# Joint layer-norm steps with their inverse roots on POOL

## The chip, the cores and the metric

The kernel runs on one core of a Trainium2 chip. The metric is device time in microseconds for one execution: the median of three runs before the change is 1777.33 us (1776.58 to 1781.38).

## What is computed

The input is 8 sequences of 2048 tokens with 256 features, float32. Three residual sublayers follow each other:

```python
x = x + 0.5 * ffn(layernorm(x), w1, b1, w2, b2)
x = x + s4d(layernorm(x), ...)        # a long convolution, then a layer norm of its own
x = x + 0.5 * ffn(layernorm(x), w1, b1, w2, b2)
```

`ffn` is `relu(x @ w1 + b1) @ w2 + b2` with an inner width of 1024, and `layernorm(x)` is `(x - mean) / sqrt(var + 1e-5)` over the 256 features of a token. Every layer norm therefore needs one inverse root for every token.

## The kernel before, in words

The 16384 tokens are split into 64 groups of 256 tokens (two tiles of 128 tokens, one token to a partition). The work runs in three stages: the first feed-forward sublayer with tag `a` (until some 800 us), the convolution, and the second feed-forward sublayer with tag `b`. In a feed-forward sublayer a group has eight slots, one for each 128 columns of the inner width. In a slot TensorE runs six "up" matmuls into `ph` (L856, each product split into a high and a low part of the operands), ACT makes `hx` by a relu (L928), DVE makes its low part (L116 on `hx`), and three slots later TensorE runs six "down" matmuls from `hx` into `po` (L866).

A group has a `pre` part before its up matmuls and a `post` part behind its down matmuls. Both are generators that the loop `sublayer` advances by one step in each slot; a bare `yield` in them is thus a wait of one slot. `pre` starts 18 slots ahead of the group's first up matmul in stage `a`. It loads `xa`, takes mean and variance on DVE (`bn_stats`, `bn_aggr` into `mv`), normalises into `xn` on ACT (L730), and turns `xn` by 128x128 transposes on TensorE (L794), or for some groups by two DMAs, into `xh` and `xl`, which the up matmuls read. POOL adds the output bias to `xa` (L777).

`post` of stage `a` adds `po` to `xa` and makes the second layer norm of the same rows, into `u`, for the convolution. The `post` of group g and the `pre` of group g+3 come together in time. From group 3 on they share one "joint" step (61 of them): one `mv` tile of 128x4 holds the mean and variance of both, and the inverse root is taken once for the four columns: a root on ACT (L704, `s_u`), then on DVE a reciprocal (L714), two steps that refine it (L116, `q_u`), a second reciprocal (L717) and the shift `nb_u` (L116). ACT's norms of `xn` and `u` (L730) read `t_u` and `nb_u`. Three numbers of a joint say in which slot, counted from `post`, the root, the refinement and the norm come: 2, 3, 4 for groups turned by DMA, else 3, 4, 6. In this text joint j is the one of `post` group j and `pre` group j+3.

Beside the matmuls of stage `a`, the tables for the convolution are built as background work: `matrices` with its inner `powers` (L490 to L497), `lags` (L536 to L570) and `make` (L600 to L610) put 285 multiplications, additions and small DMAs on POOL, most of them on tiles of 128x512, until about 568 us; ACT and DVE copy the tables (L620, L646) and SP moves them. After that POOL runs a scan (L1110 to L1113).

The order on each engine is not the order of the source alone. A scheduler that plans with its own timeline places each instruction, and each engine then takes its instructions strictly in that order. `keep_in_program_order` ties an instruction behind the one that was traced before it on the same engine; an instruction that is not tied may be placed on either side of it.

Of the kernel before, what the change touches and what calls it, by code (L numbers as in the profile page):

```python
# [10 lines left out]
F32 = mybir.dt.float32  # L11
# [4 lines left out]
ALU = mybir.AluOpType  # L16
# [3 lines left out]
P = 128  # L20
EPS = 1e-5
# [22 lines left out]
def macaron_s4d_kernel(  # L44
# [18 lines left out]
    V = nc.vector  # L63
    A_ = nc.scalar
    G_ = nc.gpsimd
# [10 lines left out]
    NTB = 2  # L76
    TOK = NTB * P
    NG = NJ * B // NTB
# [20 lines left out]
    const = ctx.enter_context(tc.tile_pool(name="const", bufs=1))  # L99
    stat = ctx.enter_context(tc.tile_pool(name="stat", bufs=4))  # L100
# [14 lines left out]
    def stt(o, a, s, b, op0, op1):  # L115
        return V.scalar_tensor_tensor(out=o, in0=a, scalar=s, in1=b, op0=op0, op1=op1)  # L116
# [10 lines left out]
    u = upool.tile([P, NQ, H, CQ], F32, name="u")  # L127
# [16 lines left out]
    hb2 = const.tile([P, H], F32, name="hb2")  # L144
    eps4 = const.tile([P, 1], F32, name="eps4")
    V.memset(eps4, 0.25 * EPS)
    A_.activation(stat.tile([P, 1], F32, name="warm", tag="s"), eps4, AF.Sqrt)

    W1Q = [nc.sync] * 4
# [536 lines left out]
    def moments(n, name):  # L686
        return stat.tile([P, n, 2], F32, name=f"mv_{name}", tag=f"mv{n}")

    def stats(srcs, name, pin=False, mv=None):
        st = stat.tile([P, NTB, 6], F32, name=f"st_{name}", tag="st")  # L690
        mv = moments(NTB, name) if mv is None else mv
        for i, src in enumerate(srcs):
            ins = V.bn_stats(st[:, i, :], src)
            if pin:
                tc.keep_in_program_order(ins)
        for i in range(NTB):
            V.bn_aggr(mv[:, i, :], st[:, i, :])
        return mv

    def root(mv, name):  # L700

        n = mv.shape[1]
        s = stat.tile([P, n], F32, name=f"s_{name}", tag=f"s{n}")
        root_[0] = A_.activation(s, mv[:, :, 1], AF.Sqrt, bias=eps4, scale=0.25)  # L704
        return s

    root_ = [None]

    def rstds(mv, s, name):

        n = mv.shape[1]
        t = stat.tile([P, n], F32, name=f"t_{name}", tag=f"tt{n}")
        q = stat.tile([P, n], F32, name=f"q_{name}", tag=f"q{n}")
        V.reciprocal(t, s)  # L714
        stt(q, mv[:, :, 1], EPS, t, ALU.add, ALU.mult)
        stt(q, q, 0.25, s, ALU.mult, ALU.add)
        V.reciprocal(t, q)  # L717
        return t

    def shifts(mv, rs, name):  # L720
        nb = stat.tile([P, mv.shape[1]], F32, name=f"nb_{name}", tag=f"nb{mv.shape[1]}")
        stt(nb, mv[:, :, 0], -1.0, rs, ALU.mult, ALU.mult)
        return nb

    def norm(dsts, srcs, mv, rs, name, on_act=False, nb=None, pin=False):
        if on_act and nb is None:
            nb = shifts(mv, rs, name)
        for i, (dst, src) in enumerate(zip(dsts, srcs)):
            if on_act:
                ins = A_.activation(  # L730
                    dst, src, AF.Identity, bias=nb[:, i : i + 1], scale=rs[:, i : i + 1]
                )
                if pin:
                    tc.keep_in_program_order(ins)
            else:
                V.tensor_scalar(dst, src, mv[:, i, 0:1], rs[:, i : i + 1], ALU.subtract, ALU.mult)
# [9 lines left out]
    def ucols(g):  # L746
        return [column(g * NTB + i) for i in range(NTB)]

    def halves(xt):
        return [xt[:, i, :] for i in range(NTB)]  # L750
# [215 lines left out]
    class Joint:  # L966
# [3 lines left out]
        def __init__(self, g, by_dma):  # L970
            self.mv = moments(2 * NTB, f"j{g}")

            self.root_at, self.rstd_at, self.norm_at = (2, 3, 4) if by_dma else (3, 4, 6)

    joints = {}
    JG = 3
# [13 lines left out]
    def post_a(g, po):  # L990
        xt = xts.pop(g)
        V.tensor_add(xt, po, xt)
        nc.sync.dma_start(out=x1_dram[:, g * NTB : (g + 1) * NTB, :], in_=xt)
        joint = joints.pop(g, None)
        mv = stats(halves(xt), f"u{g}", mv=joint.mv[:, NTB:] if joint else None)
        whole = joint.mv if joint else mv
        for _ in range(joint.root_at if joint else 1):
            yield
        s = root(whole, f"u{g}")
        if joint or g == NG - 1:  # L1000
            tc.keep_in_program_order(root_[0])
        for _ in range(joint.rstd_at - joint.root_at if joint else 1):
            yield
        rs = rstds(whole, s, f"u{g}")
        nb = shifts(whole, rs, f"u{g}")
        if joint:
            joint.rs, joint.nb = rs, nb
            rs, nb = rs[:, NTB:], nb[:, NTB:]

        for _ in range(joint.norm_at - joint.rstd_at + 1 if joint else 1):  # L1010
            yield
        for i in range(NTB):
            norm(
                ucols(g)[i : i + 1], [xt[:, i, :]], mv[:, i : i + 1], rs[:, i : i + 1], f"u{g}_{i}",
                g < ACT_NORM, nb[:, i : i + 1], True,
            )
            yield
        posted[0] = g + 1
# [199 lines left out]
    def begin():  # L1218
        for _ in range(sizes[1] // PB):
            next(head)  # L1220

    sublayer(
        w1t, w2t, pre_a, post_a, 18, "a", load_weights(), chain(matrices(), early()),
        {"half": NG // 2, "tables": NG * 3 // 4},
        {NG * SLOTS - 6: lambda: next(head), NG * SLOTS - 1: begin},
# [127 lines left out]
```

## Time and profile before

| | |
|---|---|
| median of the runs | 1777.33 us |
| the profiled execution | 1773.09 us, its span 1771.3 us |
| busy share of the span | PE 98%, DVE 78%, ACT 56%, POOL 33% |
| POOL busy from 200 to 400 us | 169.11 of 200 us |
| POOL busy from 600 to 800 us | 48.84 of 200 us |
| mean granted TensorE clock | 0.992 |

A row of a group reads: line, engine, operation, written tile <- read tiles, shape, count, then the time that the engine was busy with them, the mean duration of one in ns, and the idle time of the engine just ahead of them with what ended it. A row of the timeline reads: start, duration, engine, line, operation, tiles, shape, count, and in brackets the idle time before it. A row of the windows reads: the stretch, its length, then for each engine the busy time and the number of instructions, the granted TensorE clock, the share of the DMA engines and GB/s.

### The profile page before, as it was taken

What the parts mean: (1) busy time and instruction counts of PE and PEld (TensorE: products, weight loads), DVE (VectorE), ACT (ScalarE), POOL (GpSimd) and SP (SyncE); (2) the same over time, 40 slices, a digit from 0 to 9 for tenths busy, and PEclk for the clock granted to TensorE, in tenths of its full rate; (3) what the DMA queues carried; (4) which work ended last, traced back from release to release, by engine and by line L of the source; (5) the groups of instructions that cost most, each with busy time, mean ns of one, the idle gap of its engine ahead of it and who ended that gap; (6) DMA issues with size and microseconds to landing.
All of it is one profiled execution on the core that took longest, in us unless ns stands there. A gap on an engine that the chain in (4) does not pass through costs nothing. (4 is left out here: it accounts for less than half of the span.)

```text
span 1771.3 us, 41152 instructions
## 1 busy us (share of the span) xinstructions
PE 1729.9 (98%) x15411; PEld 1701.7 (96%) x15411; DVE 1373.3 (78%) x4415; ACT 997.8 (56%) x2188; POOL 591.5 (33%) x548
## 2 busy tenths in 40 slices
PE   8999999999999999999999899999999999999998
PEld 7999899999999999999999789999999999999998
DVE  6998777677766766766999678887788788888874
ACT  4554567667777755543555445555555555555553
POOL 1116979976776115110000122222222222222220
PEclk9999999999999999999999989999999999999999
DMA  5111266679877643335888913333333333333331
GB/s 194 43 49 40 72 203 209 192 214 288 249 233 238 173 114 94 93 108 170 260 268 260 290 49 90 94 92 91 90 96 96 90 88 93 90 96 96 90 96 49
DMA packets 299407, 245.33 MB, mean 139 GB/s; under 512 B 169924, under 2 KB 242372, under 8 KB 298694
## 3 DMA queue, kind: packets, MB, share of 16 engines
q1 hardware_dynamic: 297456, 241.75, 46.5%
q8 instruction: 121, 1.98, 0.5%
q0 software_dynamic: 768, 0.66, 0.2%
q14 instruction: 80, 0.66, 0.1%
q10 hardware_dynamic: 982, 0.27, 0.1%
HBM read 91.89 MB, written 111.15 MB: 115 GB/s over the span
## 5 line engine op out<-in xcount | busy, mean ns | idle before, releaser
L866 PE MATMUL po_a<-wa,hx_a 128*128 128x256 f32 x3072 | 455.8, 285 | 12.8 <-DVE hx_a L116 12.6
L856 PE MATMUL ph_a<-xh_a,wa 128*128 128x256 f32 x2048 | 455.1, 287 | 1.8 <-ACT xh_a L803 1.4
L856 PE MATMUL ph_b<-xh_b,wb 128*128 128x256 f32 x2048 | 444.9, 285 | 3.5 <-ACT xh_b L803 3.5
L866 PE MATMUL po_b<-wb,hx_b 128*128 128x256 f32 x3072 | 441.3, 283 | 0.1
L866 PEld LDWEIGHTS po_a<-wa,hx_a 128*128 128x128 f32 x3072 | 406.3, 193 | 15.9 <-DVE hx_a L116 15.1
L866 PEld LDWEIGHTS po_b<-wb,hx_b 128*128 128x128 f32 x3072 | 401.0, 192 | 0.3 <-DVE hx_b L116 0.3
L856 PEld LDWEIGHTS ph_a<-xh_a,wa 128*128 128x128 f32 x2048 | 356.1, 193 | 4.9 <-ACT xh_a L803 1.8
L856 PEld LDWEIGHTS ph_b<-xh_b,wb 128*128 128x128 f32 x2048 | 354.4, 194 | 4.1 <-ACT xh_b L803 4.1
L928 ACT ACTIVATE hx_b<-ph_b 128x256 fp32r<-128x256 f32 x512 | 193.8, 383 | 263.6 <-PE ph_b L856 249.6
L928 ACT ACTIVATE hx_a<-ph_a 128x256 fp32r<-128x256 f32 x512 | 192.9, 387 | 212.9 <-PE ph_a L856 206.0
L116 DVE SCALAR_TENSOR_TENSOR hx_a<-ph_a,hx_a 128x256 fp32r<-128x256 f32 x512 | 207.9, 412 | 129.1 <-ACT hx_a L928 127.7
L856 PE MATMUL ph_a<-xl_a,wa 128*128 128x256 f32 x1024 | 291.6, 286 | 3.4 <-DVE xl_a L837 3.1
L856 PE MATMUL ph_b<-xl_b,wb 128*128 128x256 f32 x1024 | 286.4, 285 | 0.0
L116 DVE SCALAR_TENSOR_TENSOR hx_b<-ph_b,hx_b 128x256 fp32r<-128x256 f32 x512 | 211.8, 415 | 66.9 <-ACT hx_b L928 61.5
L1288 POOL TENSOR_TENSOR xb<-xb,lnb_sb 128x512 f32<-128x512 f32 x64 | 82.5, 1292 | 502.1 <-DMA xb<-x_dram 332.4
L856 PEld LDWEIGHTS ph_a<-xl_a,wa 128*128 128x128 f32 x1024 | 198.2, 194 | 4.7 <-DVE xl_a L837 3.7
L856 PEld LDWEIGHTS ph_b<-xl_b,wb 128*128 128x128 f32 x1024 | 198.5, 194 | 0.2 <-DVE xl_b L805 0.2
L777 POOL TENSOR_TENSOR xa<-xa,hb 128x512 f32<-128x512 f32 x64 | 88.9, 1389 | 270.8 <-ACT xn L730 259.6
L777 POOL TENSOR_TENSOR xb<-xb,hb 128x512 f32<-128x512 f32 x64 | 94.6, 1477 | 62.5 <-ACT xn L730 31.8
L730 ACT ACTIVATE xn<-xb,nb_fb,t_fb 128x255 f32<-128x255 f32 x127 | 69.4, 594 | 75.4 <-DVE nb_fb L116 74.2
L815 DVE COPY pl_b<-xn 128x512 uint16<-128x512 uint16 x62 | 39.8, 642 | 74.8 <-ACT xn L730 74.8
L730 ACT ACTIVATE u<-xa,nb_u,t_u 128x256 f32<-128x256 f32 x104 | 89.9, 865 | 0.0
(262 smaller groups left out, 2537.8 us busy)
## 6 DMA issues: line engine op xcount, KB each, us to landing
xa<-in_L_attn_x_dram SPq DMA_DIRECT2D x64, 256.0 KB, 3.1
x_dram<-xa SPq DMA_DIRECT2D x64, 256.0 KB, 2.5
o<-u SPq DMA_DIRECT2D x32, 512.0 KB, 3.6
pv<-planes SPq DMA_DIRECT2D x32, 512.0 KB, 3.5
pt<-u SPq DMA_DIRECT2D x32, 512.0 KB, 3.9
tz<-kpad SPq DMA_DIRECT2D x64, 256.0 KB, 4.5
xb<-x_dram SPq DMA_DIRECT2D x64, 256.0 KB, 2.8
out_dram<-xb SPq DMA_DIRECT2D x64, 256.0 KB, 2.9
```

The costliest lines, as they stand in the source:

```text
L116: return V.scalar_tensor_tensor(out=o, in0=a, scalar=s, in1=b, op0=op0, op1=op1)
L730: ins = A_.activation(dst, src, AF.Identity, bias=nb[:, i : i + 1], scale=rs[:, i : i + 1])
L777: return G_.tensor_add(xt, xt, hb2.unsqueeze(1).to_broadcast([P, NTB, H]))
L815: copy(pl[:, w], xu[:, :, :, :, w])
L856: nc.tensor.matmul(ph, wt[wp][:, dc, fs], xp[:, dc, :], start=(n == 0), stop=(n == 3 * NDC - 1))
L866: nc.tensor.matmul(po[:, i, :], hp[:, tsl], wt[wp][:, fc, :], start=(fc == 0 and i == 0 and n == 0), stop=(fc == NFC - 1 and n == 2), skip ...
L928: last[A_] = A_.activation(hh, ph, AF.Relu)
L1288: G_.tensor_add(xt, xt, lnb_sb.unsqueeze(1).to_broadcast([P, NTB, H]))
```

## The change

The joint steps no longer use ACT's root or DVE's five small operations. Four operations on POOL take their place: add epsilon to the variances, raise to the power -1/2 with a constant 128x4 tile `power`, multiply by the means, and multiply by -1. All four are tied to the program order. The step comes in slot 1 (groups turned by DMA) or 2 after `post`, where the root came in slot 2 or 3; the norm stays in slot 4 or 6, and the later norm of `u` stays in its slot too. Norm steps outside the 61 joints keep the root on ACT.

```diff
+    power = const.tile([P, 2 * NTB], F32, name="power")
+    V.memset(power, -0.5)
...
+    def powers_of(mv, name):
+
+        n = mv.shape[1]
+        t = stat.tile([P, n], F32, name=f"t_{name}", tag=f"tt{n}")
+        nb = stat.tile([P, n], F32, name=f"nb_{name}", tag=f"nb{n}")
+        pin = tc.keep_in_program_order
+        pin(G_.tensor_scalar_add(t, mv[:, :, 1], EPS))
+        pin(G_.tensor_tensor(t, t, power, op=ALU.pow))
+        pin(G_.tensor_mul(nb, mv[:, :, 0], t))
+        pin(G_.tensor_scalar_mul(nb, nb, -1.0))
+        return t, nb
...
-            self.root_at, self.rstd_at, self.norm_at = (2, 3, 4) if by_dma else (3, 4, 6)
+            self.rstd_at, self.norm_at = (1, 4) if by_dma else (2, 6)
...
-        whole = joint.mv if joint else mv
-        for _ in range(joint.root_at if joint else 1):
-            yield
-        s = root(whole, f"u{g}")
-        if joint or g == NG - 1:
-            tc.keep_in_program_order(root_[0])
-        for _ in range(joint.rstd_at - joint.root_at if joint else 1):
-            yield
-        rs = rstds(whole, s, f"u{g}")
-        nb = shifts(whole, rs, f"u{g}")
+        for _ in range(joint.rstd_at if joint else 1):
+            yield
         if joint:
-            joint.rs, joint.nb = rs, nb
+            rs, nb = joint.rs, joint.nb = powers_of(joint.mv, f"u{g}")
             rs, nb = rs[:, NTB:], nb[:, NTB:]
+        else:
+            s = root(mv, f"u{g}")
+            if g == NG - 1:
+                tc.keep_in_program_order(root_[0])
+            yield
+            rs = rstds(mv, s, f"u{g}")
+            nb = shifts(mv, rs, f"u{g}")
```

In the changed program the four operations stand at L728 to L731, the up matmuls at L870, the down matmuls at L880, the relus at L942, the norms at L744, the bias additions at L791 and the tables at L492 to L612.

More of the change, by code (lines that the diff above doesn't have):

```diff
@@ L995, in post_a @@
         mv = stats(halves(xt), f"u{g}", mv=joint.mv[:, NTB:] if joint else None)
-        whole = joint.mv if joint else mv
-        for _ in range(joint.root_at if joint else 1):
+        for _ in range(joint.rstd_at if joint else 1):
             yield
-        s = root(whole, f"u{g}")
-        if joint or g == NG - 1:
-            tc.keep_in_program_order(root_[0])
-        for _ in range(joint.rstd_at - joint.root_at if joint else 1):
-            yield
-        rs = rstds(whole, s, f"u{g}")
-        nb = shifts(whole, rs, f"u{g}")
-        if joint:
-            joint.rs, joint.nb = rs, nb
-            rs, nb = rs[:, NTB:], nb[:, NTB:]
+        if joint:
+            rs, nb = joint.rs, joint.nb = powers_of(joint.mv, f"u{g}")
+            rs, nb = rs[:, NTB:], nb[:, NTB:]
+        else:
+            s = root(mv, f"u{g}")
+            if g == NG - 1:
+                tc.keep_in_program_order(root_[0])
+            yield
+            rs = rstds(mv, s, f"u{g}")
+            nb = shifts(mv, rs, f"u{g}")
         for _ in range(joint.norm_at - joint.rstd_at + 1 if joint else 1):
```

## The prediction

> **What bounds the kernel now.** I read the page first, then TensorE's waits, then the windows by stage, then the groups of DVE and POOL, and last the timeline around single joints.
>
> ```profile
> PE 1729.9 (98%) x15411; PEld 1701.7 (96%) x15411; DVE 1373.3 (78%) x4415; ACT 997.8 (56%) x2188; POOL 591.5 (33%) x548
> POOL 1116979976776115110000122222222222222220
> ```
>
> TensorE is busy for 98% of the span, so a gain can come only out of its 41 us of idle time. POOL is at 33% on average, but its row of slices shows where: nearly full from the fourth to the thirteenth slice, almost empty after.
>
> ```profile
> PE po_a L866 <- DVE hx_a L116: 12.6, 9, 2.6
> PE pt_b L794 <- ACT xn L730: 7.5, 2, 7.4
> ```
>
> The largest wait (12.6 us in 9 pieces) is for DVE's low part of `hx`; the next is at the start of the last stage, where no joint runs.
>
> ```profile
> 200.00:400.00 200.00, 190.90 (x1566) 188.46 (x1564) 149.65 (x366) 131.49 (x256) 169.11 (x163) 0.99 0.62 189
> 600.00:800.00 200.00, 200.00 (x1724) 197.49 (x1723) 133.25 (x434) 110.55 (x259) 48.84 (x72) 1.00 0.37 105
> ```
>
> TensorE (third number) idles 9.1 us from 200 to 400 us and nothing from 600 to 800 us. POOL (the fifth engine) is busy for 169 us of the first stretch. So whatever the joints cost or save shows in the first half of stage `a`, while POOL builds the tables; behind it TensorE leaves no time to win.
>
> **What is removed.** The five DVE operations of a joint, first from 100 to 600 us, then one of them from 600 to 800 us:
>
> ```profile
> L116 DVE SCALAR_TENSOR_TENSOR q_u<-mv_j,t_u 128x4 f32<-128x4 f32 x40 | 27.6, 690 | 0.6
> L116 DVE SCALAR_TENSOR_TENSOR q_u<-q_u,s_u 128x4 f32<-128x4 f32 x40 | 19.3, 482 | 0.5
> L116 DVE SCALAR_TENSOR_TENSOR nb_u<-mv_j,t_u 128x4 f32<-128x4 f32 x40 | 16.1, 403 | 0.6
> ...
> L116 DVE SCALAR_TENSOR_TENSOR q_u<-mv_j,t_u 128x4 f32<-128x4 f32 x16 | 2.7, 169 | 0.5
> ```
>
> The same operation on four elements takes 690 ns beside a busy POOL and 169 ns beside an idle one: those with two inputs wait out a POOL operation. With the two reciprocals (6.8 and 6.3 us) the change takes 76.1 us off DVE in that stretch, 1.9 us a joint, and 0.3 us of root off ACT. On the path of this stand at most TensorE's gaps there: between 150 and 400 us I count 16.0 us in 13 gaps, nearly all ended by DVE's `hx_a` or `xl_a`, and some plainly behind a `q_u` (1.90 us at 186.21, then a gap of 2.40 us at 187.58). That is the most that can be won, 0.9% of the time.
>
> **What is added: four POOL operations for each of 61 joints.** The nearest rows:
>
> ```profile
> L602 POOL TENSOR_TENSOR u<-u 128x512 f32<-128x512 f32 x32 | 36.0, 1128 | 1.7
> L610 POOL TENSOR_TENSOR u<-u 128x512 f32<-128x512 f32 x32 | 43.1, 1346 | 1.9
> L1112 POOL TENSOR_TENSOR xsE<-xsE,te 128x128 f32<-128x128 f32 x14 | 6.7, 476 | 0.1
> L143 POOL MEMSET xn<- 128x2 f32 x1 | 0.1, 101 | 0.0
> ```
>
> A line through 1128 ns at 512 elements and 476 ns at 128 gives 0.27 us at 4; the ends are 0.10 us (the memset) and 0.48 us. For the power the trace has nothing: I bound it by 0.10 us below and by 2.0 us above, a POOL row of 1024 elements, and take twice a plain operation, 0.55 us. A joint then costs POOL 3 x 0.27 + 0.55 = 1.4 us (0.4 to 3.4). None of it is a gain for POOL, which had no part in a joint.
>
> [...]
>
> **What is moved: the joint now stands in POOL's queue.** This weighs more than the price of the four. The order in which the changed program's instructions stand is known. POOL around joint 25, and TensorE where group 28 begins:
>
> ```
> L572 kpad<-u        L728 t_u         L572, L612 u<-u     L729 t_u
> L602, L608, L604    L730 nb_u        L606 u<-u           L731 nb_u
>
> L870 ph_a_7 (group 27, six)   L880 po_a <- hx_a_4, hx_a_5, hx_a_6, hx_a_7   L870 ph_a_0 (group 28)
> ```
>
> Three things follow. First, the four are not one after another: the scheduler fills the waits between them with table operations, here L572, L612, L602, L608, L604 and L606, each above 1 us but the first. Second, the last of the four of joint 25 stands behind 191 table operations. Third, the scheduler itself sees the norm come late: before the change three slots of down matmuls are still outstanding when a group's first up matmul comes, and now none are left at groups 14, 15, 16, 17, 20, 22, 23, 25 and 28 (before: 1 to 3 at each). There TensorE has no matmul of the sublayer left to run. On ACT the norm of joint 25 now stands behind 223 relus of stage `a`, not 217; that of joint 13 behind 128, which are all relus of the groups ahead of the one that waits for it.
>
> On top of that the chip's POOL runs behind this order. In the trace of before:
>
> ```profile
> 366.59 1.09 ACT L730 ACTIVATE xn<-xa,nb_u,t_u 128x255 f32<-128x255 f32 x2 [2.94 <-DVE nb_u L116]
> ...
> 377.21 0.38 ACT L928 ACTIVATE hx_a<-ph_a 128x256 fp32r<-128x256 f32 x1 [0.99 <-PE ph_a L856]
> ...
> 386.54 1.06 POOL L606 TENSOR_TENSOR u<-u 128x512 f32<-128x512 f32 x1
> 387.55 1.29 POOL L610 TENSOR_TENSOR u<-u 128x512 f32<-128x512 f32 x1
> ```
>
> The first row is joint 25's norm, at 366.6. The second is group 28's first relu, so its first up matmul ran near 376.2. The last row is POOL's 191st table operation: it ended at 388.8. From a norm to the end of `xl` the trace takes 4.2 to 5.4 us where TensorE turns the tile; with 4.5 us, group 28 could begin at 393.3, 17.1 us late, before POOL has done one new operation. The same count gives 6.8 us at joint 13, 9.5 at 17, 12.0 at 22, 14.6 at 26, 12.7 at 27, and nothing from joint 32 on. These are not added up: a stall at joint 13 lets POOL catch up for the later ones, so the largest counts, 17 us. Before the change the same lag cost nothing, since only L791's bias addition (then L777), needed a whole group later, stood in that queue.
>
> **The sum.** Lag of the queue: +17 us. New POOL work up to joint 27: joints 10 to 27 are 18 x 1.4 = 25 us; POOL idles 40.8 us of the 252.5 us from 160 to 412.5, in pieces that end by a transfer, DVE or ACT; these absorb delay, but move with a stalled TensorE, so I let half of them (20 us) absorb: +5 us (with the ends 0.4 and 3.4: 0 to +41). Saved: twelve of the 13 gaps lie ahead of group 28's late start and inside the lag, so only the last, 2.62 us at 399.63, counts: -2 us. After 600 us POOL is free, the four take 1.4 us where DVE and ACT took 2.6 us from `mv` to `nb`, and TensorE had no gap: 0. Together +20 us: 1793 us against the profiled 1773.09 us. The median of the runs lies 4.2 us above the profiled one, so 1797 us.
>
> Queued behind the new waits: on POOL the tables and bias additions, on ACT, whose norm now waits for POOL, the relus that free `ph` and feed the down matmuls, the table copies, and through them SP's transfers.
>
> **Rivals.** (1) POOL keeps up. Without the joints' operations in its way DVE frees buffers sooner, POOL's 40.8 us of idle time shrink, and the 191st operation comes 17 us earlier; then the 16 us of gaps go too: 1777 - 16 to 1777 - 9, some 1764 us. For it: DVE's stalls are real. Against it: of its eleven idle pieces over 0.5 us in that stretch six end by a `pt` transfer or by ACT, which this does not quicken, and the order has the drained groups written in. It decides if POOL reaches joint 25 by 371.7. Chance 0.08. (2) The two cancel: the drained groups cost what the gaps gave back, within 5.3 us, which is the 0.3% that a measurement of this kernel can tell from no change. Chance 0.08. (3) The power is slow: at 2 us a joint costs 2.8 us, 18 of them 50 us, and with 20 absorbed +30 instead of +5: 1822 us; above 2 us POOL becomes the bound until 568 us and each microsecond more costs 18 us or over. Nothing in the trace speaks against it. Chance 0.15. (4) The lag as summed: 0.69.
>
> **The numbers.** The forecast is 1797 us. The low end, 1780, is the lag reduced to the smallest of the later peaks with all idle absorbing; the high end, 1838, is +17 + 41 - 2 from the price of 3.4 us, and some for a slower power. Faster 0.08, same 0.08, slower 0.84.
>
> **What would show it.** Right: L729 below 1 us; ACT's `xn` waiting for POOL's `nb_u`, some 3 us and more a joint between 200 and 420 us; TensorE idle for 25 us and more from 150 to 430 us, ended by `xh_a` or `xl_a` at the first up matmul of groups 16, 20, 25 and 28; DVE's idle time up. Wrong: POOL's 191st table operation ends before joint 25's norm is due, or TensorE's idle time in that stretch falls below 16 us.

## The result, and the profile after

The changed kernel takes 1803.91 us, the median of four runs (1801.72 to 1806.40), beside 1777.2 us for the kernel before on the same chip: a ratio of 1.0145 (1.0132 to 1.0158, the 95% interval, as behind every ratio below), slower by 1.45%, some 26 us. Below, every ratio is to the kernel before measured again beside that run (1774 to 1775 us), and an effect in us is the ratio's distance from 1 times 1775 us.

The profiled execution took 1804.13 us with a span of 1801.9 us, 30.6 us over the span before. The page after:

```profile
PE 1735.7 (96%) x15411; PEld 1702.6 (94%) x15411; DVE 1301.6 (72%) x4111; ACT 985.1 (55%) x2127; POOL 690.6 (38%) x792
...
PE   8999799699999999999999979999999999999998
...
POOL 2228989897788324522000022222222222222220
```

TensorE has the same 15411 matmuls. Its idle time (span less busy) rose from 41.4 to 66.2 us, its busy time from 1729.9 to 1735.7: 24.8 us of waiting and 5.8 us of busy time make the 30.6. DVE lost 304 operations and 72 us, and the kernel is slower all the same. POOL has 244 operations more (4 x 61) and 99 us. In TensorE's row the fifth and eighth slices (7 and 6; a slice is 45 us) are two holes. TensorE's waits after name them:

```profile
PE pt_a L808 <- ACT xn L744: 13.5, 4, 11.4
PE ph_a L870 <- ACT xh_a L849: 10.6, 3, 9.3
PE po_a L880 <- DVE hx_a L116: 8.9, 14, 1.6
```

The columns are total us, times, longest. Before, the first was 1.0 us in all and the second was not there; the old leader, the wait for DVE's `hx`, fell from 12.6 to 8.9. Two single stalls, 11.4 and 9.3 us, are most of the added idle time. The windows after, laid out as before:

```profile
200.00:400.00 200.00, 169.98 (x1346) 165.66 (x1345) 103.66 (x261) 115.59 (x214) 181.03 (x209) 0.93 0.59 175
600.00:800.00 200.00, 197.44 (x1658) 194.72 (x1658) 129.23 (x354) 114.33 (x251) 72.66 (x130) 1.00 0.41 117
```

From 200 to 400 us TensorE idles 30.0 us where it idled 9.1, although POOL is only 11.9 us busier, and the granted clock falls from 0.99 to 0.93. From 150 to 430 us TensorE has run 1968 matmuls, before 2142; at the 8.5 matmuls a us that the kernel before makes from 430 to 800 us, the 174 missing are 20 us. The four new operations on POOL:

```profile
L729 POOL TENSOR_TENSOR t_u<-t_u,power 128x4 f32<-128x4 f32 x61 | 66.8, 1096 | 2.2
L730 POOL TENSOR_TENSOR nb_u<-mv_j,t_u 128x4 f32<-128x4 f32 x61 | 17.6, 289 | 2.1
...
L728 POOL TENSOR_SCALAR t_u<-mv_j 128x4 f32<-128x4 f32 x61 | 15.9, 261 | 184.2 <-DVE mv_j L699 181.7
```

The power takes 1.10 us on four elements, the plain ones 0.26 to 0.29 us. With L731 (0.28 us) a joint costs POOL 1.92 us of work. What it costs in time is seen in POOL's timeline at joint 13:

```profile
192.96 0.28 POOL L728 TENSOR_SCALAR t_u<-mv_j 128x4 f32<-128x4 f32 x1
...
196.82 1.06 POOL L729 TENSOR_TENSOR t_u<-t_u,power 128x4 f32<-128x4 f32 x1
197.82 1.99 POOL L498 TENSOR_TENSOR u<-u 128x1024 f32<-128x1024 f32 x1
...
208.56 0.20 POOL L730 TENSOR_TENSOR nb_u<-mv_j,t_u 128x4 f32<-128x4 f32 x1
208.71 2.40 POOL L499 TENSOR_TENSOR u<-u 128x1024 f32<-128x1024 f32 x1
...
213.60 0.23 POOL L731 TENSOR_SCALAR nb_u<-nb_u 128x4 f32<-128x4 f32 x1
```

From the start of the first of the four to the end of the last 20.9 us pass, of which the four fill 1.8. POOL is not idle in between: it runs the table operations that the scheduler put there. Past 595 us, with no tables, a joint takes 2.0 to 2.4 us from `mv` to `nb_u` (three of them 4.0 to 5.8), where ACT and DVE mostly took 2.6 before. ACT's norms of joints 13 and 22 after:

```profile
213.86 1.09 ACT L744 ACTIVATE xn<-xa,nb_u,t_u 128x255 f32<-128x255 f32 x2 [2.39 <-POOL nb_u L731]
...
355.26 1.33 ACT L648 COPY u<-planes 128x1024 uint16<-128x1024 uint16 x1 [9.20 <-DMA planes<-pv]
...
357.40 1.09 ACT L744 ACTIVATE xn<-xa,nb_u,t_u 128x255 f32<-128x255 f32 x2
```

And TensorE at groups 16 and 25, whose `pre` these joints are:

```profile
223.26 1.23 PE L870 MATMUL ph_a<-xh_a,wa 128*128 128x256 f32 x4 [9.33 <-ACT xh_a L849]
...
358.05 1.39 PE L808 MATMUL pt_a<-ident,xn 128*128 128x128 f32 x4 [11.41 <-ACT xn L744]
```

The first stall is the forecast one: a late joint, a late norm, late operands (group 16 is turned by DMA, so 9.4 us lie between the norm's start and the first matmul). The second is so only in part. Joint 22 came late too, but in another way than joint 13:

```profile
322.88 0.24 DVE L699 BATCH_NORM_AGGREGATE mv_j<-st_u 128x2 f32<-128x6 f32 x2
...
341.78 0.42 POOL L728 TENSOR_SCALAR t_u<-mv_j 128x4 f32<-128x4 f32 x2
```

It waited 18.7 us in front of the first of the four and spent 6.6 us inside them; at joint 13 it was 3.0 and 20.9 us. POOL had finished joint 22's `nb_u` at 348.3 us, but the norm stood on ACT behind a table copy (L648) that waited 9.20 us for a transfer: ACT had copied the table at 344.08 us, SP sent it out at 347.88, took it back at 350.79, and it was there at 355.2. In ACT's order no relu stood between. That this copy stood there so late because of the joints on POOL was not tested by itself; with the cheap power below the stall is 3.19 us, with less work on POOL or with tied tables at most 1.3 us.

### The profile page after: what moved, and what is told of

It reads as the page before. It is cut to its first block, busy times and chain, and to the rows that moved or that the text cites. A ratio compares the mean times of both kernels' runs of the same rounds, so it can differ in the third digit from the quotient of the medians.

```text
span 1801.9 us, 41034 instructions
## 1 busy us (share of the span) xinstructions
PE 1735.7 (96%) x15411; PEld 1702.6 (94%) x15411; DVE 1301.6 (72%) x4111; ACT 985.1 (55%) x2127; POOL 690.6 (38%) x792
## 5 line engine op out<-in xcount | busy, mean ns | idle before, releaser
L870 PE MATMUL ph_a<-xh_a,wa 128*128 128x256 f32 x2048 | 453.9, 288 | 16.3 <-ACT xh_a L849 10.6
L880 PE MATMUL po_a<-wa,hx_a 128*128 128x256 f32 x3072 | 451.5, 285 | 9.4 <-DVE hx_a L116 8.9
L870 PE MATMUL ph_b<-xh_b,wb 128*128 128x256 f32 x2048 | 444.7, 285 | 4.1 <-ACT xh_b L817 4.1
L880 PE MATMUL po_b<-wb,hx_b 128*128 128x256 f32 x3072 | 441.1, 283 | 0.0
L880 PEld LDWEIGHTS po_a<-wa,hx_a 128*128 128x128 f32 x3072 | 403.2, 192 | 13.5 <-DVE hx_a L116 11.3
L880 PEld LDWEIGHTS po_b<-wb,hx_b 128*128 128x128 f32 x3072 | 400.5, 192 | 0.0
L870 PEld LDWEIGHTS ph_a<-xh_a,wa 128*128 128x128 f32 x2048 | 355.7, 194 | 21.1 <-ACT xh_a L849 11.2
L870 PEld LDWEIGHTS ph_b<-xh_b,wb 128*128 128x128 f32 x2048 | 354.5, 194 | 4.7 <-ACT xh_b L817 4.7
L942 ACT ACTIVATE hx_b<-ph_b 128x256 fp32r<-128x256 f32 x512 | 193.4, 382 | 265.0 <-PE ph_b L870 253.1
L942 ACT ACTIVATE hx_a<-ph_a 128x256 fp32r<-128x256 f32 x512 | 191.6, 387 | 237.1 <-PE ph_a L870 213.7
L870 PE MATMUL ph_a<-xl_a,wa 128*128 128x256 f32 x1024 | 291.6, 287 | 2.9 <-DVE xl_a L851 2.5
L870 PE MATMUL ph_b<-xl_b,wb 128*128 128x256 f32 x1024 | 286.3, 285 | 0.0
L870 PEld LDWEIGHTS ph_a<-xl_a,wa 128*128 128x128 f32 x1024 | 199.0, 194 | 5.6 <-DVE xl_a L851 3.7
L870 PEld LDWEIGHTS ph_b<-xl_b,wb 128*128 128x128 f32 x1024 | 198.6, 194 | 0.0
L791 POOL TENSOR_TENSOR xb<-xb,hb 128x512 f32<-128x512 f32 x64 | 94.1, 1470 | 56.6 <-ACT xn L744 36.9
L744 ACT ACTIVATE xn<-xb,nb_fb,t_fb 128x255 f32<-128x255 f32 x127 | 69.6, 595 | 71.5 <-DVE nb_fb L116 71.4
L791 POOL TENSOR_TENSOR xa<-xa,hb 128x512 f32<-128x512 f32 x64 | 85.4, 1334 | 57.8 <-ACT xn L744 57.5
L695 DVE BATCH_NORM_STATS2 st_fa<-xa 128x6 f32<-128x256 f32 x128 | 49.5, 418 | 66.5 <-DMA xa<-in_L_attn_x_dram 66.4
```

Source lines behind the costliest of these rows:

```text
L744: ins = A_.activation(dst, src, AF.Identity, bias=nb[:, i : i + 1], scale=rs[:, i : i + 1])
L791: return G_.tensor_add(xt, xt, hb2.unsqueeze(1).to_broadcast([P, NTB, H]))
L870: nc.tensor.matmul(ph, wt[wp][:, dc, fs], xp[:, dc, :], start=(n == 0), stop=(n == 3 * NDC - 1))
L880: nc.tensor.matmul(po[:, i, :], hp[:, tsl], wt[wp][:, fc, :], start=(fc == 0 and i == 0 and n == 0), stop=(fc == NFC - 1 and n == 2), skip ...
L942: last[A_] = A_.activation(hh, ph, AF.Relu)
```

## The experiments

My theory before the runs: the lag of POOL's queue costs the time, in part through the table operations inside the four. Its rivals: the power's price; lags that add up from joint to joint; DVE time freed that brings nothing because DVE never bound anything.

**The power's price.** One run gives the power the cost of a plain multiplication, so its factors are not inverse roots; one does the power twice.

```diff
-        pin(G_.tensor_tensor(t, t, power, op=ALU.pow))
+        pin(G_.tensor_tensor(t, t, power, op=ALU.mult))     # e1_cheap
```
```diff
         pin(G_.tensor_tensor(t, t, power, op=ALU.pow))
+        pin(G_.tensor_tensor(nb, t, power, op=ALU.pow))     # e1_double
```

> The power is replaced by a multiplication by the same tile, so the norms get wrong factors; everything else is as in the changed kernel, though the scheduler plans the shorter operation and places it anew. In the changed kernel the power took 1.10 us and a plain operation of 128x4 0.28 us, so POOL loses about 0.8 us a joint, 27 us over the 33 joints that run beside the tables. Queue theory (the joint stands behind POOL's tables, and the tables stand behind the joints): part of the loss stays, 1785 to 1797 us, with drained groups still at 15, 16, 23, 25 and 28. Price theory (the power alone fills POOL): the loss is gone, 1777 us or below.

> A second power of the same size is put in behind the first, into a tile that is written over later: 1.1 us more on POOL a joint, 36 us over the 33 joints beside the tables. Both theories see POOL as the bound there: 1815 to 1840 us if little of it finds idle time. If the loss came from the order of the tied operations alone, whatever they cost: 1804 us.

Cheap: 1784.45 us, 1.0054 (1.0038 to 1.0070), +10 us. Double: 1814.93 us, 1.0221 (1.0199 to 1.0242), +39 us. Both lie less than 1 us under the lower edge that was expected of the queue. From the +26 of the change that is 16 us less and 13 us more. In the cheap run the operation changed by 0.83 us (L729 now 0.27 us); times the 18 joints from 10 to 27 this is 15 us, so there the price comes through whole. The second power of 1.11 us makes 20 us in the same count, of which 13 came. The price is not all: without it the stall of group 16 is still there, and longer. TensorE's waits of e1_cheap:

```profile
PE ph_a L870 <- ACT xh_a L849: 13.9, 2, 13.0
```

**Only where no tables are built.** Joints 9 to 41 keep the old path, the others use POOL.

```diff
+            self.on_pool = not 9 <= g <= 41     # else root, rstds, shifts as before
```

> Roots on POOL only in the joints 0 to 8 and 42 to 60, that is while POOL builds no tables; the joints 9 to 41 keep ACT's root and DVE's small operations in their old slots. Queue theory: no loss, 1772 to 1780 us, and TensorE's idle time from 150 to 430 us as before the change (16 us). If every joint lost by its longer way over POOL, wherever it stands: 28 of 61 joints would bring 12 of the 27 us, 1789 us.

1774.53 us, 0.9991 (0.9980 to 1.0001): no difference, as the queue theory expected. The window of e2_outside shows TensorE idle 11.2 us, near the 9.1 before:

```profile
200.00:400.00 200.00, 188.76 (x1556) 185.91 (x1554) 150.03 (x366) 132.48 (x258) 168.92 (x163) 1.00 0.62 191
```

The loss thus comes from the joints 9 to 41, which run beside the tables, and the others neither cost nor bring anything that can be told from nothing.

**Is an early lag paid once?** POOL takes over from joint 15 on only, so joint 13 is the old one.

```diff
+            self.on_pool = g >= 15     # else root, rstds, shifts as before
```

> Roots on POOL from joint 15 on; joints 0 to 14 keep ACT's root and DVE's small operations, so that the joints beside the powers stage, joint 13 among them, are as before the change. If the lags are not added up and the largest alone counts, the stall of 9.3 us at group 16 is gone but comes back at later groups: 1798 to 1806 us. If each joint's lag costs by itself, the 9 us and joint 14's share are saved: 1788 to 1795 us.

1796.28 us, 1.0125 (1.0109 to 1.0140), +22 us: only 4 us of the 26 go, though joint 13's stall of 9.33 us goes. In its place stand later ones of 2.54, 5.02 and 5.68 us. In us the result lies between the two expectations. They were set against a kernel before of 1777 us; with the ratio that is 1799 us, inside the first. The intervals of the two ratios overlap (1.0132 to 1.0158 after), so little of the early stall is saved for certain: the reading that it lets POOL catch up for the later ones fits, on one kernel whose order was planned anew.

**The four kept together.** The table multiplications, additions and subtractions on POOL are tied to the program order too, to keep them out from between the four; POOL's small DMAs and the bias additions are not tied. As this ties the tables as well, the same edit on the kernel before is the control.

```diff
+    class Tied:
+        def __getattr__(self, name):
+            f = getattr(G_, name)
+            return lambda *a, **k: tc.keep_in_program_order(f(*a, **k))
+    GT = Tied()
...
-                G_.tensor_mul(nr, re, w_r)
+                GT.tensor_mul(nr, re, w_r)
...
-            E = G_
+            E = GT
```

> The changed kernel, with every table operation on POOL tied to the program order too, so that no table operation that was traced later can slip between the four of a joint, and none traced earlier can be passed. If the table operations between the four are what makes a joint late (up to 14 of them at joint 13), the joints get their factors within 3 us of their turn and the loss shrinks: 1780 to 1795 us. If it is the backlog in front of the first of the four, nothing is won, and less freedom for the scheduler costs: its order has no down matmul outstanding at ten group boundaries from 18 to 27, so 1805 to 1825 us.

> A control: the kernel before the change, with the same table operations tied to the program order on POOL. There no joint stands in POOL's queue. If the gain of tying in the changed kernel came from keeping the four of a joint together: no change here, 1772 to 1780 us. If tying speeds up the tables by itself: some 1755 us, 20 us less, as much as it brought there.

e3_tied: 1781.84 us, 1.0040 (1.0027 to 1.0054), +7 us. The control: 1773.94 us, 0.9995 (0.9983 to 1.0007), nothing. So tying takes off some 19 of the 26 us, and gives none of it where no joint stands in POOL's queue. POOL's timeline of e3_tied at joint 13:

```profile
190.51 0.23 POOL L735 TENSOR_SCALAR t_u<-mv_j 128x4 f32<-128x4 f32 x1 [1.32 <-DVE mv_j L706]
190.81 1.04 POOL L736 TENSOR_TENSOR t_u<-t_u,power 128x4 f32<-128x4 f32 x1
191.93 0.20 POOL L737 TENSOR_TENSOR nb_u<-mv_j,t_u 128x4 f32<-128x4 f32 x1
192.22 0.38 POOL L738 TENSOR_SCALAR nb_u<-nb_u 128x4 f32<-128x4 f32 x1
```

The four now take 2.1 us where they took 20.9, with the same power at the same price. They are not kept together everywhere: at joint 24 four small DMAs and a table operation still stand between them, and they take 10.8 us. The wait in front of the first grows instead, to between 10 and 18 us at joints 17 to 26. The gaps of TensorE from 280 to 400 us are 2.3 us or less, but there are many, and the table of matmuls below shows what they cost.

**Was there anything to win on DVE?** Both runs edit the kernel before and leave out the refinement of the root: the first doubles the root and takes one reciprocal, the second takes an unscaled root with epsilon as its bias and one reciprocal.

```diff
+        if n == 2 * NTB:                     # e6_norefine, in rstds
+            V.tensor_scalar_mul(s, s, 2.0)
+            V.reciprocal(t, s)
+            return t
```
```diff
+        if n == 2 * NTB:                     # e8_plainroot, in root (bias eps1 = EPS, scale 1.0)
+            root_[0] = A_.activation(s, mv[:, :, 1], AF.Sqrt, bias=eps1, scale=1.0)
+            return s
...
+        if n == 2 * NTB:                     # in rstds
+            V.reciprocal(t, s)
+            return t
```

> The kernel before the change, with the two DVE operations q_u of the joints left out: the inverse root is the reciprocal of ACT's root, doubled first, without the refinement. Of the three DVE operations with two inputs that waited for POOL in a joint one (nb_u) stays. If DVE's waits for POOL made TensorE's 16 us of gaps between 150 and 400 us, most of them go: 1763 to 1770 us. If the gaps come from DVE's other work (table copies, copies of the turned tiles), little moves: 1774 to 1778 us.

> The kernel before the change, with a joint's root unscaled on ACT, so that the inverse root is one reciprocal on DVE and nothing else; the refinement is left out. Against the run that doubled the root first it drops one more DVE operation, which took 459 ns on average from 100 to 600 us though it has one input. If each DVE operation that waits for POOL counts: 1 to 4 us less than the 1766 us of that run, 1762 to 1766 us. If the remaining gaps come from nb_u alone, the same 1766 us.

e6_norefine: 1766.25 us, 0.9954 (0.9937 to 0.9971), -8 us. So the small DVE operations do hold TensorE; that rival falls. e8_plainroot: 1769.73 us, 0.9967 (0.9954 to 0.9979), -6 us: taking away one more operation gave nothing more, and the two intervals overlap. That is the second of its expectations, that what is left comes from the shift, which stays and waits (607 ns on average in that run). Groups of e6_norefine on DVE from 100 to 600 us:

```profile
L116 DVE SCALAR_TENSOR_TENSOR nb_u<-mv_j,t_u 128x4 f32<-128x4 f32 x40 | 28.2, 705 | 0.5
L714 DVE TENSOR_SCALAR s_u<-s_u 128x4 f32<-128x4 f32 x39 | 17.9, 459 | 1.0 <-ACT s_u L704 1.0
```

With the `q_u` gone `nb_u` went from 403 to 705 ns: in both kernels the first two-input operation of the chain takes longest (690 ns for the first `q_u` before, 705 for `nb_u` here).

**Less work on POOL.** Two of the operations of `make`, a subtraction and an addition, 64 instructions in all, go from POOL to DVE; on the changed kernel and, as control, on the one before. Then both edits at once.

```diff
-            E.tensor_sub(pr, pr, tm)
+            V.tensor_sub(pr, pr, tm)
...
-            E.tensor_add(pi, pi, tm)
+            V.tensor_add(pi, pi, tm)
```

> The changed kernel, with the subtraction and the addition of make (64 of its 192 operations, 1.06 to 1.35 us each) on DVE instead of POOL. Queue theory: POOL loses some 75 us of table work from 200 to 570 us, twice what the joints brought there, so the loss after group 17 goes; the stall at group 16 lies before it and stays: 1780 to 1792 us. If DVE, which takes the 64 operations and waits for POOL in each, becomes the one that is late: above 1800 us.

> A control: the kernel before the change with the subtraction and addition of make on DVE. POOL's load sets nothing there and DVE gets more work that waits for POOL: 1777 to 1790 us. If less load on POOL helps by itself, through shorter waits of DVE: 1765 to 1775 us.

> The changed kernel with both remedies: the table operations tied, so that the four of a joint stay together, and the subtraction and addition of make on DVE, so that the backlog in front of a joint is shorter. Tying alone left 7 us of loss, the move alone 5 us, and each left what the other treats: backlog waits of 11 to 15 us at joints 19 to 24, or the stall of 10 us at group 16. Queue theory: both go, and DVE's small operations are still saved: 1762 to 1772 us, below the kernel before. If DVE, with 64 more operations that wait for POOL, gives back what it saved: 1772 to 1782 us.

e5_make_dve: 1779.52 us, 1.0028 (1.0016 to 1.0040), +5 us; the stall of group 16 is still 10.09 us long, the later long ones are gone. The control e5_make_dve_b: 1763.12 us, 0.9943 (0.9928 to 0.9958), -10 us, a miss: I had expected DVE to suffer. The kernel gained, and DVE's rows fit the reason that a less busy POOL holds DVE less, which no run shows apart from the other things that the edit moves. DVE's groups of e5_make_dve_b from 100 to 600 us:

```profile
L116 DVE SCALAR_TENSOR_TENSOR q_u<-mv_j,t_u 128x4 f32<-128x4 f32 x41 | 15.1, 367 | 0.3
```

This row was 690 ns before. Against this control the joints on POOL still cost e5_make_dve some 15 us. e11_tied_make, the joints on POOL with both edits: 1757.51 us, 0.9917 (0.9900 to 0.9933), -15 us, the fastest of all, faster than the kernel before, and 4 us under what was expected at best. Its window:

```profile
200.00:400.00 200.00, 195.77 (x1630) 194.38 (x1629) 155.21 (x355) 142.07 (x259) 170.56 (x203) 1.00 0.75 222
```

TensorE idles 4.2 us there, before 9.1, after 30.0. Most of the gain is the moved table work, which gives 10 us by itself. That the joints on POOL add the other 5 us is not shown: the two intervals overlap, and the kernel before with both edits was not run.

**Where each run loses.** Counting TensorE's matmuls places the loss. Each row says when, in the profiled execution of the kernel before, so many matmuls had started, and how many us later (+) or earlier (-) the other profiled executions were at the same count:

| matmuls | before, us | after | e3_tied | e5_make_dve | e11_tied_make | e5_make_dve_b |
|---|---|---|---|---|---|---|
| 1400 | 186.5 | -2.6 | -3.0 | -2.9 | -2.7 | -0.5 |
| 1700 | 230.6 | +5.4 | -11.1 | +8.3 | -10.9 | -2.5 |
| 2100 | 280.7 | +8.3 | -7.6 | +9.2 | -10.4 | -0.9 |
| 2900 | 382.8 | +24.3 | +9.3 | +4.4 | -16.3 | -6.8 |
| 4000 | 518.6 | +22.8 | +6.9 | +0.1 | -18.6 | -11.3 |
| 4900 | 626.9 | +28.8 | +8.0 | +4.0 | -17.5 | -8.5 |

There are two losses with two causes (the last column is the control of e5_make_dve). The first lies at joints 13 and 14, between the first two rows, and of the edits in the table only tying removes it: it is what stood inside the four. Of the some 21 us between the two kernels at the end of stage `a` 16 are there by 2100 matmuls, and none are added up to 4000. The second lies from 2100 to 2900 matmuls, some 16 us in the changed kernel and 17 us in the tied one, whose joints wait 10 to 18 us in front there: the backlog. Moving table operations off POOL removes it, tied (e11_tied_make, waits of at most 4.6 us at joints 15 to 28) or not (e5_make_dve); there both go at the pace of their control. The tied plan has ten group starts with no down matmul outstanding, from group 18 to 27, most of them in that second stretch. A last 6 us of the changed kernel, between 4000 and 4900 matmuls, as the tables end, are not explained.

## Why the prediction was right, step by step

The sign, the place and the main mechanism held: POOL's queue beside the tables, TensorE waiting at the first up matmuls of a few groups, nothing lost by joints outside the tables (e2_outside). The forecast of 1797 us was 7 us short, within its range, but its terms were not all right, and that their sum came so near is in part luck.

- **Lag of the queue, +17.** The 17 us were taken from group 28, where the measured wait is 0.92 us. The stall at group 16 was put at 6.8 us and measured 9.33; at group 25 there was one of 11.41 us, and 1.21 us at group 20. So the size is right for a reason that was not forecast: two losses, of 8 us by 1700 matmuls against 1400 and 16 us from 2100 to 2900, and not one largest lag. The second is the backlog that the step meant. The first is mostly what lies inside the four, 20.9 us at joint 13; the text named that interleaving and gave it no price of its own.
- **The drained groups** fit the second loss, in the changed kernel and in e3_tied, but the plan alone gave no size: the changed kernel starts group 28 0.92 us late and group 25 11.41.
- **New work on POOL, +5.** Three plain operations at 0.27 us each were right (0.26 to 0.29), the power at 0.55 was half of the 1.10 measured, so 18 joints are 18 x 1.92 = 34.6 us, not 25. POOL's idle time from 150 to 430 us fell by 24 us (from 45.7 to 21.4), where half of it, 20, was taken to absorb. By that step's own rule the term is 35 - 20 = 15, not 5; with the 24 it is 11 and the total 26, as measured. That agreement is a coincidence: e1_cheap takes off 16 us with the power alone, so the two terms overlap and do not add as they were written. The rival of the slow power put 2 us on it, double what it takes.
- **Saved, -2.** e6_norefine shows that DVE's gaps were real and worth some 8 us. The changed kernel is 2.6 us ahead at 1400 matmuls, and the tied one 11.1 us at 1700, so the saving is there until the losses come; the wait for `hx_a` fell from 12.6 to 8.9 us in all.
- **After 600 us: 0.** A joint mostly takes 2.0 to 2.4 us there from `mv` to `nb_u`, a little less than before, though the four themselves take 1.92 and not 1.4. TensorE idles 2.6 us from 600 to 800 us after, and none before, and between 4000 and 4900 matmuls 6 us are lost in all. e2_outside, with the late joints on POOL, loses nothing, so those joints by themselves are not the cause; in the changed kernel the tables also end 27 us later. It is not settled further.
- **ACT waiting for `nb_u`, 3 us and more a joint** was wrong. The whole wait is 27.4 us in 19 pieces, none above 3.3 us, and only 4.1 us of it from 200 to 420 us. ACT had other work first, or another wait.
- **Missing: the second path.** The prediction named the table copies only among what waits behind the norm. At group 25 it went the other way: the norm waited behind a table copy for a transfer.
- **Missing: busy time.** 5.8 of the 30.6 us in the profiled executions are busy time, which a sum made of idle time alone cannot hold. It is not the clock: from 150 to 430 us TensorE was busy at half clock for 11.0 us after and 9.7 us before, over the whole span for 23.9 and 23.4. From 430 to 800 us, at a granted clock of 1.00 in both, it made 8.3 matmuls in a busy us after and 8.5 before; what that is, short waits that count as busy or another mix of matmuls, stays open.

The test of L729 below 1 us failed by 0.1 us; TensorE's idle time from 150 to 430 us was 33.6 us, above the 25 set as the mark (before 16.1), but of the four groups named only 16 and 25 had a large wait.

## What to carry to other kernels

POOL ran the changed kernel's instructions in the planned order (joint 25's stand in its timeline, from 386.01 to 396.92 us, as the prediction listed them). There a chain of dependent small operations costs what stands between them, 20.9 us at joint 13 for 1.8 us of work, so before moving such a chain look up in the changed order what the scheduler puts inside it, and keep the neighbours tied as well as the chain. Price the in-between operations apart from the backlog in front, and treat both: here tying removed the first and 19 of the 26 us, the backlog went on costing 17 us until POOL had less to do, and with both gone the same move was part of the fastest version. A large stall shows one loss; a count of work done against time shows also the loss that is spread over many small gaps. When DVE's small two-input operations wait beside a busy POOL (690 ns on average where they take 169 beside an idle one), moving other work off POOL can bring more than moving the small operations: here it brought 10 us, and the move of the small ones alone cost 26.

## What the hardware showed that was not expected

**The clock after a stall.** Windows of the changed kernel behind the two stalls; the granted clock is the first number without brackets behind the five engines:

```profile
223.00:228.00 5.00, 4.74 (x26) 4.74 (x27) 1.54 (x3) 1.93 (x6) 4.83 (x9) 0.61 0.02 3
226.00:227.00 1.00, 1.00 (x6) 1.00 (x6) 0.42 (x1) 0.34 (x2) 0.92 (x3) 0.53 0.00 0
...
358.00:363.00 5.00, 3.48 (x14) 2.80 (x15) 0.69 (x1) 4.44 (x6) 4.43 (x4) 0.50 0.47 177
363.00:368.00 5.00, 5.00 (x29) 5.00 (x29) 3.08 (x12) 4.78 (x10) 4.70 (x7) 0.61 0.75 274
...
366.00:367.00 1.00, 1.00 (x7) 1.00 (x7) 0.91 (x7) 1.00 (x4) 0.70 (x3) 0.56 0.23 85
367.00:368.00 1.00, 1.00 (x11) 1.00 (x10) 0.50 (x2) 1.00 (x2) 1.00 (x2) 1.00 0.53 122
368.00:373.00 5.00, 5.00 (x45) 5.00 (x44) 1.47 (x4) 2.01 (x5) 5.00 (x6) 1.00 0.99 299
```

After 9.33 us of idle the mean clock of the next 5 us is 0.61, with 26 matmuls; after 11.41 us it is 0.50 and then 0.61 in two such stretches, with 14 and 29, against 45 at full clock. The short windows show that the clock was near one half until shortly before 227 and 367 us and full after, 3.7 us after work began at 223.26 and 6.0 us after it became steady at 360.89. A shorter gap was followed by half clock too, and two that were shorter still were not. Windows of the kernel before behind gaps of 1.93, 1.81 and 2.62 us, which end at 157.42, 245.20 and 402.25 us:

```profile
157.42:160.29 2.87, 2.87 (x24) 2.87 (x24) 2.84 (x6) 0.38 (x1) 2.12 (x2) 1.00 0.04 16
245.20:248.07 2.87, 2.87 (x23) 2.79 (x24) 1.83 (x4) 0.77 (x2) 2.72 (x4) 1.00 0.79 254
402.25:405.12 2.87, 2.87 (x13) 2.87 (x14) 2.87 (x11) 0.30 (x1) 2.79 (x3) 0.50 1.05 303
```

So the gap of 2.62 us, with 13 matmuls behind it in a time that holds 23 or 24 at full clock, cost more than its length, which the prediction's count of gaps left out.

**The power on POOL.** 1.10 us on 128x4 where a multiplication takes 0.27 us on the same tiles (L729 of e1_cheap).

**DVE operations with one input can wait for POOL too.** In e6_norefine a multiplication by a constant on 128x4 took 459 ns from 100 to 600 us and 156 ns from 600 to 800 us, when POOL was a quarter busy. A reciprocal of the same shape took 162 to 177 ns throughout. What the multiplication waited for these means do not show. In the timeline of the kernel before single rows show it for two `q_u` and for a copy, which has one input:

```profile
182.96 1.11 POOL L496 TENSOR_TENSOR u<-u 128x512 f32<-128x512 f32 x1
183.14 0.95 DVE L116 SCALAR_TENSOR_TENSOR q_u<-mv_j,t_u 128x4 f32<-128x4 f32 x1
...
184.02 1.98 POOL L490 TENSOR_TENSOR u<-u 128x1024 f32<-128x1024 f32 x1
...
184.35 1.97 DVE L833 COPY xf_a<-pt_a 128x512 uint16<-128x512 uint16 x1
...
185.95 2.15 POOL L494 TENSOR_TENSOR u<-u 128x1024 f32<-128x1024 f32 x1
186.21 1.90 DVE L116 SCALAR_TENSOR_TENSOR q_u<-q_u,s_u 128x4 f32<-128x4 f32 x1
```

Each `q_u` ends within 0.02 us of the end of a POOL operation (184.09 and 184.07, 188.11 and 188.10). The copy ends 0.32 us behind one; it took 1.97 us, and on average 0.49 us from 600 to 800 us. From 100 to 600 us 57 of the 120 `q_u` and `nb_u` of joints took more than 0.3 us, and each of the 57 ended within 0.03 us of the end of a POOL operation.
